# Cross attention's scores in waves of four banks, and its products in two halves of the queries

## The chip, the cores and the metric

The kernel runs on one core of one Trainium2 chip. The metric is the device time of one execution in microseconds (us). Times are medians of several runs. A profile is one execution taken by the hardware profiler. Its engines are PE (TensorE, the matrix engine; PEld is its loading of weights), DVE (VectorE), ACT (ScalarE), POOL (GpSimd) and SP (SyncE, which issues DMAs). A difference under about 0.2% (3.5 us) can't be told from none.

## What is computed

Two decoder layers over x (4 sequences, 512 positions, 256 features) with a context of 4 x 1601 x 128, all in float32. Each layer adds self attention, then cross attention, then a feed-forward block, with a layer norm behind each. The change lies in the second layer's cross attention, which has 16 heads of 16 features:

```python
qh = (q @ Wq + bq).reshape(B, LQ, HEADS, D_K).transpose(0, 2, 1, 3)
kh = (k @ Wk + bk).reshape(B, LKV, HEADS, D_K).transpose(0, 2, 1, 3)
vh = (v @ Wv + bv).reshape(B, LKV, HEADS, D_K).transpose(0, 2, 1, 3)
scores = jnp.einsum('bhqd,bhkd->bhqk', qh, kh) * scale
attn = jax.nn.softmax(scores, axis=-1)
out = jnp.einsum('bhqk,bhkd->bhqd', attn, vh)
concat = out.transpose(0, 2, 1, 3).reshape(B, LQ, D_MODEL)
return concat @ Wo + bo
```

Here `q` is x and `k`, `v` are the context, so each head has 512 queries and 1601 keys. The last feed-forward block is a tree of 255 gates and 256 leaves per position.

## The kernel before

The program has three parts, one behind the other: `front` (first layer's attentions), `experts` (first layer's feed-forward) and `heads` (the whole second layer). Each part is written as nodes of a **plan**: a node has an engine, a cost in us, a priority, the nodes it depends on and the buffers it takes. `Plan.run` is a list scheduler at build time. It keeps a model time for each engine, always places the node that can start first (within 0.05 us the one of lowest priority number), and writes the instructions in that order. So the order in each engine's queue is the plan's; the chip then waits for semaphores in that order. `hold` is a node that only takes a buffer, in turn.

For PE the plan tells three modes apart. `row` nodes are scores: a head has 16 features, padded to 32 rows of the array, and four heads lie on four row strips (lanes j = 0 to 3), so four score matmuls can run at once. `col` nodes are products of weights and values: four heads on four column strips. All other matmuls fill the whole array (`full`). `Plan.turn` (L89) decides between them: after `BURST` = 4 row nodes in a row it prefers something else, if that is ready, and after `AWAY` = 0.8 us of something else it goes back to rows.

The work is cut into groups of four heads: 4 batches x 4 groups for self attention, then as many for cross attention. `head_group` (L1050) writes one group of cross attention in two passes:

- **maxima** (L1088 to L1131). For each of 4 query tiles and each of 3 runs of 512 keys, and for each of the 4 heads, one score matmul of 32 x 512 into one PSUM bank of the pool `one` (L1098 to L1100), which DVE reduces to a maximum per query (L1106). That is 48 score matmuls and 48 reductions in a group. The 65 keys that are left go as one node of 16 small matmuls into four banks (`rest`, L1120 to L1127), with four reductions (L1129). Then the chain of the shift: the largest of them (L1134), its negative (L1137), a transpose by PE (L1142) and an addition to the queries, which makes `qa` (L1146).
- **weights and products** (L1154 to L1199). For each of 13 tiles t of keys and each of the 4 heads, one score matmul of the shifted queries into one bank (L1168), and ACT's exponential into one of ten buffers `pe` (L1173). When the four heads of a tile are there, `product` (L1187 to L1199) adds four matmuls of 512 queries to the one accumulator bank `acc` (L1190). That is 52 scores, 52 exponentials and 13 products in a group. At the end ACT copies `acc` to `o` (L1204), and PE transposes it (L1210).

The next group's exponentials depend on its own `hold` of `acc` (L1150, L1164), so the plan places them after that copy. The maxima of later groups don't depend on it.

In the program every float32 matmul is two PE instructions (two passes), so four score matmuls are 8 instructions in the profile, and so are the four matmuls of a product. All helper matmuls are recorded at L245, the products at L1190.

PSUM has eight banks here: seven in the pool `one`, one as `acc`. `one` also serves every other matmul of this part: projections of queries, keys and values (L972 to L1048), two transposes a group, and per batch the output projection with its norm (L1242, L1283) and the tree (L1333). Queries and keys go to their lanes by DMAs on SP's queue (L1066), into 2 buffers `qT` and 3 buffers `kT`.

Of the kernel before, what the change touches and what calls it, by code (L numbers as in the profile page):

```python
# [11 lines left out]
ALU = mybir.AluOpType  # L12
# [34 lines left out]
class Node:  # L47
    def __init__(self, eng, cost, prio, fn, deps, take, lanes, mode):
        self.cost = dict(zip(eng.split("|"), cost if isinstance(cost, tuple) else (cost,)))
        self.eng, self.prio, self.fn = eng, prio, fn  # L50
        self.deps, self.take, self.lanes, self.mode = deps, take, lanes, mode
        self.releases, self.users, self.slot = [], 0, None
        self.start = self.end = self.on = None


class Plan:
# [2 lines left out]

    SLACK, LOOK, BURST, AWAY, IDLE = 0.05, 96, 4, 0.8, 0.5
    LAT = {"pe": 0.25, "act": 0.1, "dve": 0.08, "pool": 0.1, "none": 0.0, "sp": 0.5, "dma": 1.5}

    def __init__(self):
# [2 lines left out]
    def pool(self, name, n):  # L68
        self.pools[name] = [0.0] * n
# [7 lines left out]
    def hold(self, name, pr, deps=()):  # L77

        before = self.turns.get(name)
        n = self.add("none", 0.0, pr, None, [*deps, *([before] if before else [])], take=[name])  # L80
        self.turns[name] = n
        return n

    def frees(self, n, those):
# [16 lines left out]
    def run(self, tc):  # L101
# [12 lines left out]
        with tc.manual_schedule():  # L114
            while todo:
                best = None
                for queue in ready.values():
                    queue.sort(key=lambda n: (n.prio, n.i))
                    options = []
                    for n in queue[: self.LOOK]:  # L120
                        s = max([d.end + self.LAT[d.on] for d in n.deps], default=0.0)
                        ok = True
                        for p in n.take:
                            times = [t for t in self.pools[p] if t is not None]
                            if not times:
                                ok = False
                                break
                            s = max(s, min(times))
                        if not ok:
                            continue  # L130
                        on = n.eng
# [22 lines left out]
                for p in n.take:  # L154
                    times = [(t, i) for i, t in enumerate(self.pools[p]) if t is not None]
                    n.slot = min(times)[1]
                    self.pools[p][n.slot] = None
                if on == "pe":
                    if n.mode == "row":
                        burst, away = burst + 1, 0.0  # L160
                    else:
                        burst, away = 0, away + n.cost[on]
                    for x in n.lanes or range(4):
                        row[x] = n.end
                    last, mode = s, n.mode
                elif on != "none":
                    free[on] = n.end
# [15 lines left out]
def cost_mm(n):  # L183

    return n * 4 / 2400


def act(n):
    return 0.1 + n * 0.833e-3


def dve(n):
    return 0.16 + n * 1.05e-3
# [11 lines left out]
def tile_decoder(ctx: ExitStack, tc: tile.TileContext, a, out):  # L205
# [38 lines left out]
    def mm(out, lhsT, rhs, c=0, n=1):  # L244
        nc.tensor.matmul(out, lhsT, rhs, start=c == 0, stop=c == n - 1)  # L245
# [666 lines left out]
    def heads():  # L912
        plan = Plan()
        with tc.tile_pool(name="h1", bufs=1) as h1, \
# [135 lines left out]
            def head_group(cross, b, g, pos, vals, pair, after):  # L1050
# [33 lines left out]
                else:  # L1084
                    for kqs in MQ:
                        units += [(j, 0, [(kq, 0, (kq + 1) * P) for kq in kqs]) for j in range(4)]
                maxes, scored = [], []
                for i, (j, m, prods) in enumerate(units):  # L1088
                    pu = pos - 1.2 + (i + 0.5) / len(units)
                    js = slice(32 * j, 32 * j + 32)  # L1090
# [10 lines left out]

                    def largest(n, s=s, j=j, m=m, at=at):
                        for kq, k0, k1, w in at:
                            t = ONE[s.slot][:, w : w + k1 - k0]
                            if cross:
                                nc.vector.tensor_reduce(MX[mx.slot][:, kq, j, m : m + 1], t, AX.X, ALU.max)  # L1106
                            else:
                                nc.vector.tensor_tensor_reduce(  # L1108
                                    out=junk[:, : k1 - k0], in0=t, in1=m_qk[:, 384 - kq * P : 512],
                                    scale=1.0, scalar=NEG, op0=ALU.add, op1=ALU.max,  # L1110
                                    accum_out=MX[mx.slot][:, kq, j, 0:1])

                    maxes.append(N("dve", sum(dve(k1 - k0) for _, k0, k1 in prods), pu, largest, [s], free=[s]))
                    scored.append(s)
                if cross:

                    pu, w = pos - 0.2, LC - 1536
                    banks = [hold("one", pu, scored[-4::]) for j in range(4)]

                    def rest(n, w=w):  # L1120
                        for kq in range(4):
                            for j in range(4):
                                js = slice(32 * j, 32 * j + 32)
                                mm(ONE[banks[j].slot][:, kq * w : (kq + 1) * w], QT[q.slot][js, kq * P : (kq + 1) * P],
                                   KT[k.slot][js, 1536:])

                    s = N("pe", cost_mm(4 * w), pu, rest, banks, lanes=(0, 1, 2, 3), mode="row")  # L1127
                    for j in range(4):
                        maxes.append(N("dve", dve(4 * w), pu, lambda n, j=j, w=w: nc.vector.tensor_reduce(  # L1129
                            MX[mx.slot][:, :, j, 3:4], ONE[banks[j].slot][:, : 4 * w].rearrange("p (a n) -> p a n", a=4),  # L1130
                            AX.X, ALU.max), [s], free=[banks[j]]))  # L1131
                pm_ = pos - 0.22
                m, nm, qa = hold("m", pm_), hold("nm", pm_), hold("qa", pm_)
                nn = N("dve", 0.2, pm_, lambda n: nc.vector.tensor_reduce(  # L1134
# [19 lines left out]
                for u, ts in enumerate(turns):  # L1154

                    at, w = [], 0
                    for t in ts:
                        at.append((t, kt_size(t) if cross else P, 0 if cross else t * P, w))
                        w += L - at[-1][2]
                    exps = []  # L1160
                    for i, j in enumerate((2, 3, 0, 1)):
                        pu = pos + (u + 0.25 * i) / len(turns)
                        js = slice(32 * j, 32 * j + 32)
                        e = hold("pe", pu, [acc])  # L1164
# [3 lines left out]
                                mm(ONE[n.slot][:kn, w : w + L - q0], KT[k.slot][js, t * P : t * P + kn], QA[qa.slot][js, q0:])  # L1168

                        s = N("pe", cost_mm(w), pu, score, [e, o, *kready], take=["one"], lanes=(j,), mode="row")  # L1170

                        def weigh(n, s=s, e=e, kn=at[0][1], w=w):
                            nc.scalar.activation(PE_[e.slot][:kn, :w], ONE[s.slot][:kn, :w], AF.Exp, scale=HD**-0.5)  # L1173

                        r = N("act", act(w), pu, weigh, [s], free=[s])
                        if not cross:
                            def causal(n, e=e, at=at):
                                for t, kn, q0, w in at:
                                    d = PE_[e.slot][:, w : w + P]
                                    nc.gpsimd.affine_select(  # L1180
                                        d, d, pattern=[[1, P]], compare_op=ALU.is_ge, fill=0.0,
                                        base=0, channel_multiplier=-1)

                            r = N("pool", len(at) * pool(128), pu, causal, [r])
                        exps.append((e, r))

                    def product(n, at=at, exps=exps, u=u):  # L1187
                        for t, kn, q0, w in at:
                            for j in range(4):
                                nc.tensor.matmul(  # L1190
                                    ACC[acc.slot][32 * j : 32 * j + HD + 1, q0:],
                                    VV[v.slot][:kn, t, 4 * (g % 2) + j, :],
                                    PE_[exps[j ^ 2][0].slot][:kn, w : w + L - q0],
                                    start=t == 0, stop=u == len(turns) - 1 and t == at[-1][0],
                                )

                    pr_ = last[-1:] if last else []
                    last.append(N("pe", cost_mm(w) + 0.05 * len(at), pos + (u + 1.2) / len(turns), product,
                                  [r for _, r in exps] + vready + [emptied] + pr_, free=[x for x, _ in exps], mode="col"))  # L1199
                plan.frees(last[-1], [k, qa])  # L1200
                if g % 2:
                    plan.frees(last[-1], [v])
# [12 lines left out]
                    RS[rs.slot], ONE[po.slot].rearrange("p (k j r) -> p k j r", k=4, j=4)[:, :, :, HD]),  # L1215
                    [po])
                if g == 0:
                    head_group.cat = hold("cat", pe_)
                cat = head_group.cat

                def scaled(n):
                    nc.vector.tensor_tensor(
# [201 lines left out]
            for k, dst in enumerate((w_gate, w_leaf)):  # L1424
                def both(n, k=k):
# [5 lines left out]
                p = N("pe", cost_mm(4 * D), 0.5, both, [fw], take=["one"], free=raw[2 * k : 2 * k + 2])  # L1431
                tree_ready.append(N("act|dve", (act(L), dve(L)), 0.5, lambda n, p=p, dst=dst: copy(
                    n.on, dst.rearrange("p m n -> p (m n)"), ONE[p.slot]), [p], free=[p]))
            pos = 0.0
            for cross in (False, True):
                for b in range(NB):
                    cats = []
                    for g in range(NG):
                        if g % 2 == 0:
                            vals = values(cross, b, g // 2, pos - 2.3, done[b])  # L1440
                            pair = projections(cross, b, g // 2, pos - 2.6, done[b])
                        c, cat = head_group(cross, b, g, pos, vals, pair, done[b])
                        cats.append(c)
                        pos += 1.0
                    done[b] = finish(cross, b, pos + 0.3, cats, cat)
                    if cross:
                        tree(b, pos + (1.2 if b < NB - 1 else 0.5), done[b])
            plan.run(tc)

    heads()  # L1450
# [99 lines left out]
```

## Time and profile before

| what | value |
|---|---|
| median of three runs | 1731.38 us (1730.46 to 1731.72) |
| the profiled execution's own time | 1728.98 us |
| its span, first to last instruction | 1727.2 us |
| mean granted PE clock | 0.974 |
| first cross score reduced by DVE (L1106) | 799.7 us |
| last cross product (L1190) begins | 1685.7 us |

The span is 1.8 us shorter than that execution's own time. The first 480 us of the span hold the first layer, up to about 799 us self attention of the second layer is the main work, and from there to 1687 us cross attention with what lies between its groups; the last 40 us are the last batch's output projection, norm and tree.

How to read the views: the page's first part gives each engine's busy time. The chain of work that ended last follows, from the last instruction back, what each step waited for; in order of time it shows how long each run of work on PE lasted, as start, length, line and count. The timeline lists instructions in order of time with the idle time before them and who ended it. The table of windows gives busy times in a stretch.

### The profile page before, as it was taken

The page shows a single profiled execution, that of the slowest core. Times are in us where ns is not written, and L with a number is a line of the kernel's source. Part 1 is how long each engine was busy: PE and PEld are TensorE (multiplying, and loading weights), DVE is VectorE, ACT ScalarE, POOL GpSimd, SP SyncE. Part 2 cuts the span into 40 slices and gives each one's busy share as a digit, 9 for nine tenths or more (in the row PEclk, how much of TensorE's full clock was granted, in tenths as well). Part 3 has the DMA queues.
Part 4 walks back from the last instruction along what each step waited for, and adds up shares of the span by engine and source line. Part 5 has one row for each costly group of instructions (what it writes and reads, how often), then busy time and mean ns, then how long its engine had stood idle before and what let it go on. Part 6 is the DMA issues. An engine that isn't in the chain of part 4 may idle for free.

```text
span 1727.2 us, 28379 instructions
## 1 busy us (share of the span) xinstructions
PE 1636.8 (95%) x10756; PEld 856.2 (50%) x10756; DVE 1104.3 (64%) x2690; ACT 759.5 (44%) x1534; POOL 330.2 (19%) x503
## 2 busy tenths in 40 slices
PE   7889999999959999999999999999999999999995
PEld 4677776888834555545433334333334333343323
DVE  6998555111138876777866766776667766677715
ACT  0335551211112434434446556455554555545581
POOL 6652003432144544422000000100000000010000
PEclk8999999999979999999999999999999999999998
DMA  8101005886331000001000000000000100001000
GB/s 304 36 2 38 25 25 199 272 277 219 115 113 38 25 14 19 17 16 26 14 3 11 14 13 14 7 19 14 13 14 1 26 14 14 13 1 26 1 1 13
DMA packets 41275, 87.50 MB, mean 51 GB/s; under 512 B 7856, under 2 KB 26800, under 8 KB 38064
## 3 DMA queue, kind: packets, MB, share of 16 engines
q1 hardware_dynamic: 32304, 42.66, 9.1%
q0 software_dynamic: 8832, 43.00, 7.3%
q8 instruction: 86, 1.41, 0.3%
q14 instruction: 53, 0.43, 0.1%
HBM read 64.52 MB, written 8.26 MB: 42 GB/s over the span
## 4 chain that ended last, share of the span: by engine, by line
PE 65%; DVE 4%; ACT 1%; issue 1%; DMA 1%; POOL 0%; DVEq 0%; POOLq 0%; ACTq 0%
PE one L245 48%; PE acc L1190 14%; DVE junk L1108 2%; PE one L1210 1%; PE one L1142 1%; PE one L1272 1%; ACT w_sgu L1173 0%; PE one L1291 0%; DMA y<-ys_dram,dest 0%; DVE x L1257 0%; DVE lst L1249 0%; DMA ys_dram<-ye 0%; PE one L1381 0%; DVE y L1308 0%; DVE rt L1373 0%
## 5 line engine op out<-in xcount | busy, mean ns | idle before, releaser
L1106 DVE TENSOR_REDUCE mx<-one 128x1 f32<-128x512 f32 x768 | 486.4, 683 | 190.0 <-PE one L245 185.7
L245 PE MATMUL one<-qa,kT 32*128 32x512 f32 (+4 forms) x2176 | 515.4, 598 | 6.2 <-ACT w_sgu L1173 4.2
L245 PE MATMUL one<-kT,qT 32*128 32x512 f32 (+4 forms) x2560 | 502.2, 529 | 6.2 <-DVE mx L1106 2.6
L1173 ACT ACTIVATE w_sgu<-one 128x512 f32<-128x512 f32 (+2 forms) x510 | 278.6, 591 | 244.8 <-PE one L245 242.7
L245 PEld LDWEIGHTS one<-qa,kT 32*128 32x128 f32 (+1 forms) x2176 | 179.6, 182 | 204.3 <-issue 68.9
L245 PEld LDWEIGHTS one<-kT,qT 32*128 32x128 f32 x2560 | 190.6, 184 | 168.3 <-issue 47.9
L1190 PE MATMUL acc<-w_sgu,v 128*17 128x512 f32 (+4 forms) x1084 | 261.9, 566 | 0.0
L1173 ACT ACTIVATE pe<-one 128x512 f32<-128x512 f32 (+1 forms) x342 | 189.8, 602 | 102.2 <-PE one L245 101.6
L1278 POOL TENSOR_TENSOR x<-x,rows 128x1024 f32<-128x1024 f32 x12 | 28.3, 2361 | 808.3 <-PE one L1272 808.2
L1190 PE MATMUL acc<-pe,v 128*17 128x512 f32 (+1 forms) x748 | 179.5, 566 | 0.0
L1108 DVE CUSTOM_DVE_ANT_0 junk<-one,consts 128x128 f32<-128x128 f32 (+3 forms) x256 | 125.4, 490 | 35.1 <-PE one L245 12.0
L1190 PEld LDWEIGHTS acc<-w_sgu,v 128*17 128x17 f32 (+1 forms) x1084 | 34.2, 96 | 176.3 <-issue 162.8
L1173 ACT ACTIVATE w_sdn<-one 128x512 f32<-128x512 f32 (+2 forms) x172 | 89.9, 568 | 63.4 <-PE one L245 63.1
L245 PEld LDWEIGHTS e_one<-xsT,wgu 128*128 128x128 f32 x768 | 89.5, 192 | 3.8 <-issue 2.9
L245 PE MATMUL e_one<-xsT,wgu 128*128 128x128 f32 x768 | 89.6, 275 | 0.0
L1190 PE MATMUL acc<-w_sdn,v 128*17 128x512 f32 (+2 forms) x344 | 84.1, 568 | 0.0
L245 PE MATMUL one<-w_in,xT 128*128 128x512 f32 (+1 forms) x128 | 47.8, 527 | 13.5 <-DMA xT<-in_xT 12.2
L245 PE MATMUL e_one<-xT,w_sgu 128*128 128x512 f32 x128 | 59.8, 609 | 0.3 <-DVE lg L613 0.3
L859 DVE TENSOR_TENSOR he<-sg,e_one 128x512 f32<-128x512 f32 x24 | 16.5, 686 | 61.6 <-PE e_one L245 51.0
L555 ACT ACTIVATE pe<-one,nm 128x512 f32<-128x512 f32 x64 | 37.3, 596 | 27.4 <-DVE nm L547 27.3
L245 PE MATMUL one<-pT,ctxN 128*128 128x128 f32 (+1 forms) x416 | 49.0, 275 | 0.0
L245 PEld LDWEIGHTS one<-pT,ctxN 128*128 128x128 f32 (+1 forms) x416 | 48.2, 192 | 1.6 <-issue 1.2
(290 smaller groups left out, 2023.3 us busy)
## 6 DMA issues: line engine op xcount, KB each, us to landing
kT<-ku SPq DMA_DIRECT2D x64, 100.1 KB
qT<-qu SPq DMA_DIRECT2D x128, 32.0 KB
ctxN<-in_ctxN SPq DMA_DIRECT2D x4, 832.0 KB
ctxT<-in_ctxT SPq DMA_DIRECT2D x4, 800.5 KB
ys_dram<-ye SPq DMA_DIRECT2D x24, 128.0 KB
xT<-in_xT SPq DMA_DIRECT2D x16, 128.0 KB
x<-in_x SPq DMA_DIRECT2D x16, 128.0 KB
x_dram<-x SPq DMA_DIRECT2D x16, 128.0 KB
```

What stands on the lines that cost most here:

```text
L245: nc.tensor.matmul(out, lhsT, rhs, start=c == 0, stop=c == n - 1)
L555: nc.scalar.activation(PE_[w.slot][:, : k1 - k0], ONE[b.slot][:, : k1 - k0], AF.Exp, bias=NM[nm.slot][:, 1:2], accum_out=PS[sm_.slot][:, i ...
L859: h = N("dve", dve(512), pr, lambda n, s=s, p=banks[1], he=he: nc.vector.tensor_tensor(HE[he.slot].rearrange("p j t -> p (j t)"), SG[s.slo ...
L1106: nc.vector.tensor_reduce(MX[mx.slot][:, kq, j, m : m + 1], t, AX.X, ALU.max)
L1108: nc.vector.tensor_tensor_reduce(out=junk[:, : k1 - k0], in0=t, in1=m_qk[:, 384 - kq * P : 512], scale=1.0, scalar=NEG, op0=ALU.add, op1=A ...
L1142: nc.tensor.transpose(ONE[n.slot][:, kq * P : (kq + 1) * P], NM[nm.slot][:, kq].rearrange("p j r -> p (j r)"), ident)
L1173: nc.scalar.activation(PE_[e.slot][:kn, :w], ONE[s.slot][:kn, :w], AF.Exp, scale=HD**-0.5)
L1190: nc.tensor.matmul(ACC[acc.slot][32 * j : 32 * j + HD + 1, q0:], VV[v.slot][:kn, t, 4 * (g % 2) + j, :], PE_[exps[j ^ 2][0].slot][:kn, w : ...
L1210: nc.tensor.transpose(ONE[n.slot][:, kq * P : (kq + 1) * P], OO[o.slot][:, kq * P : (kq + 1) * P], ident)
L1272: nc.tensor.transpose(ONE[n.slot][:, kq * P : (kq + 1) * P], XB[b][:, kq, c * P : (c + 1) * P], ident)
L1278: rw = N("pool", pool(1024), pos, lambda n: nc.gpsimd.tensor_tensor(XB[b], XB[b], rows[:, row : row + D].unsqueeze(1).to_broadcast([P, 4, ...
```

## The change

- **Waves.** Cross attention's scores are no longer nodes of one bank and one lane. A *wave* is one PE node of four score matmuls on four lanes into four banks. In the usual wave two matmuls are the shifted scores of two heads of one tile (for ACT's exponentials) of group i, and two are maxima scores of two heads (for DVE) of group i + 1 or i + 2. `head_group` becomes a generator that yields what it wants, and `wave` joins two requests.
- **The order of the waves is written out by hand**: for each group i, 18 waves of (i, i + 1), the 65 keys left of i + 1 as a wave of its own, one wave of two pairs of exponentials of i, and 6 waves of (i, i + 2). Group 0's maxima come as 12 waves of four maxima and 3 waves of group 1's; the last group's exponentials come as 13 waves of four exponentials.
- **The plan starts a wave early**: when its fourth bank will be free within 0.4 us by the plan's clock (`EARLY`). A wave counts as four of the burst.
- **Products in two halves.** In cross attention a product node is split into queries 0 to 255 and 256 to 511: two nodes of four matmuls each. The buffers `pe` are released behind the second half.
- `AWAY` is 0.4 in place of 0.8, for all plans.
- Self attention keeps its nodes. The numbers of score matmuls, reductions and exponentials are unchanged.

The diff, cut to its core:

```diff
-    SLACK, LOOK, BURST, AWAY, IDLE = 0.05, 96, 4, 0.8, 0.5
+    SLACK, LOOK, BURST, AWAY, IDLE, EARLY = 0.05, 96, 4, 0.4, 0.5, 0.4
...
+    def wave(self, cost, prio):
+        n = self.add("pe", cost, prio, None, lanes=(0, 1, 2, 3), mode="row")
+        n.parts, n.those = [], []
+        def issue(n):
+            for f, x in zip(n.those, n.parts):
+                f(x.slot)
+        n.fn = issue
+        return n
...
+                        if ok and n.parts:
+                            times = sorted(t for t in self.pools[n.parts[0].take[0]] if t is not None)
+                            ok = len(times) >= len(n.parts)
+                            if ok:
+                                s = max(s, times[len(n.parts) - 1] - self.EARLY)
...
+                for x in n.parts:
+                    p = x.take[0]
+                    t, x.slot = min((t, i) for i, t in enumerate(self.pools[p]) if t is not None)
+                    self.pools[p][x.slot] = None
+                    n.end = max(n.end, t + n.cost[on])
...
-                        burst, away = burst + 1, 0.0
+                        burst, away = burst + len(n.lanes), 0.0
...
+                if cross:
+                    for i in range(0, len(units), 2):
+                        want = []
+                        for j, m, ((kq, k0, k1),) in units[i : i + 2]:
+                            js = slice(32 * j, 32 * j + 32)
+                            want.append(lambda bank, js=js, kq=kq, k0=k0, k1=k1: mm(
+                                ONE[bank], QT[q.slot][js, kq * P : (kq + 1) * P], KT[k.slot][js, k0:k1]))
+                        s, parts = yield lambda: (want, [mx], pos - 1.2 + (i + 0.5) / len(units))
...
+                    for i in range(2 if cross else 0):
+                        pu, js2 = pos + (u + 0.5 * i + 0.25) / len(turns), (2, 3) if i == 0 else (0, 1)
...
+                        def ask():
+                            es[:] = [hold("pe", pu, [acc]) for _ in js2]
+                            return want, [*es, o, *kready], pu
+                        s, parts = yield ask
...
+                    halves = ((0, 256), (256, L)) if cross else ((0, L),)
+                    for hf, (qa0, qa1) in enumerate(halves):
...
+                        last.append(N("pe", cost_mm(w / len(halves)) + 0.05 * len(at), pos + (u + 1.2 + 0.5 * hf) / len(turns), product,
+                                      [r for _, r in exps] + vready + [emptied] + last[-1:], mode="col"))
+                    plan.frees(last[-1], [x for x, _ in exps])
...
+            AHEAD, PAIRS = 6, 24
...
+            maxima(0, PAIRS // 2)
+            wave(0, cost=cost_mm(260))
+            maxima(1, AHEAD // 2)
+            for i in range(NG * NB):
+                if i + 1 < NG * NB:
+                    for _ in range(PAIRS - AHEAD):
+                        wave(i, i + 1)
+                    wave(i + 1, cost=cost_mm(260))
+                    wave(i, i)
+                    if i + 2 < NG * NB:
+                        for _ in range(AHEAD):
+                            wave(i, i + 2)
+                    else:
+                        maxima(i, AHEAD // 2)
+                else:
+                    maxima(i, 13)
```

`cost_mm(n)` is n x 4 / 2400 us, so a wave costs 0.853 in the plan and a half of a product 0.477.

## The prediction

> **What bounds the kernel now.** I read the page first: PE is busy nearly always, the other engines are not, and the chain that ended last is PE for two thirds, nearly all of it scores (L245) and products (L1190).
>
> ```profile
> PE 1636.8 (95%) x10756; PEld 856.2 (50%) x10756; DVE 1104.3 (64%) x2690; ACT 759.5 (44%) x1534; POOL 330.2 (19%) x503
> ...
> PE 65%; DVE 4%; ACT 1%; issue 1%; DMA 1%; POOL 0%; DVEq 0%; POOLq 0%; ACTq 0%
> PE one L245 48%; PE acc L1190 14%; DVE junk L1108 2%; PE one L1210 1%; PE one L1142 1%; PE one L1272 1%; ACT w_sgu L1173 0%; PE one L1291 0%; DMA y<-ys_dram,dest 0%; DVE x L1257 0%; DVE lst L1249 0%; DMA ys_dram<-ye 0%; PE one L1381 0%; DVE y L1308 0%; DVE rt L1373 0%
> ```
>
> The table of windows puts the cross stage at 799 to 1687 us, with PE busy 878.76 of 888 us, DVE 604.68, ACT 491.37:
>
> ```profile
> 799.00:1687.00 888.00, 878.76 (x6134) 333.16 (x6126) 604.68 (x1185) 491.37 (x937) 27.13 (x57) 0.99 0.06 12
> ```
>
> But a busy PE is not a full one. The chain in order of time (start, length, what, passes) shows the pattern of a quiet stretch:
>
> ```profile
> 980.15 1.07 PE one L245 x8
> 981.23 0.98 PE acc L1190 x8
> 982.21 3.90 PE one L245 x23
> 986.11 0.98 PE acc L1190 x8
> ```
>
> Eight passes, four score matmuls on four lanes, take 1.07 us: one wave. A product takes 0.98. Then come three waves' passes (24, one of them behind the chain's cut), and they take 3.90, not 3.21. The timeline says why:
>
> ```profile
> 980.09 0.69 PE L245 MATMUL one<-qa,kT 32*128 32x512 f32 x1
> ...
> 981.24 1.09 ACT L1173 ACTIVATE w_sdn<-one 128x512 f32<-128x512 f32 x2 [1.49 <-PE one L245]
> 981.29 1.29 DVE L1106 TENSOR_REDUCE mx<-one 128x1 f32<-128x512 f32 x2 [1.14 <-PE one L245]
> ...
> 984.01 0.18 PEld L245 LDWEIGHTS one<-qa,kT 32*128 32x128 f32 x1 [0.70 <-ACT w_sgu L1173]
> ```
>
> The weight load at 984.01 waited 0.70 us for a bank: seven banks feed one wave and three quarters of the next, and a bank is free again only after ACT or DVE has drained it. I added up PE's timeline of 799 to 1687 by mode, from one run's start to the next: **rows (scores) 543 us, columns (products) 214, full 131**, together 888.
>
> **The change, part by part.** *Rows.* 48 + 52 scores in 16 groups are 1600 matmuls, 400 waves. At 1.07 each: 428. The 16 nodes of left-over keys: their 32 passes took 0.95 (1649.90 to 1650.85): 15. Rows of self attention that lie in the window, 46 passes: 6. Sum 449, against 543: **94 us of the row time is waiting**, and that is all that the change can win.
>
> *Halves.* Each of 208 products (16 x 13) becomes two. The trace has products of 256 queries, in self attention, and they take 0.56 in the chain:
>
> ```profile
> 790.49 0.56 PE acc L1190 x8
> ...
> 811.03 0.56 PE acc L1190 x8
> ```
>
> So 416 x 0.56 = 233 in place of 208 x 0.98 = 204, a cost of 29, 0.14 a product: a switch to columns and back costs the same whatever is between. Two halves that meet cost 0.98 together. How many meet? The plan puts one thing behind each wave (a wave fills the burst of 4; a half of 0.477 passes `AWAY` = 0.4). 416 waves (with the left-over ones) stand beside 416 halves and about 140 full nodes: 72 projections (9 for each of 8 pairs of groups), 32 transposes, 36 of three batch ends. So 140 things must go second into a gap, when the ten `pe` buffers run out. If these are halves: 140 x 0.14 = 20 back. I take that, 213; bound: none meet, 233. With the 10 us of columns that are self attention's and waits' today (214 less 204): **223** (bound 243).
>
> The Trainium skill has a price for this too: TensorEngine Tiling (Array Packing), section Performance Considerations, says that a matmul costs about 60 cycles beyond its columns. At the 2.4 GHz of its page TensorE: Matmul & The Clock Gate that would be, as an estimate, 25 ns, twice in a lane's half, so 10 us for 208 products in place of 29, and the result 19 us lower; the row of 0.56 is this kernel's own, and I go by it.
>
> *Bank waits that stay.* A wave that starts at 0 lets its first bank go at 1.81: ACT begins 1.15 behind the wave's start (980.09 to 981.24), one exponential lasts 0.60 (mean 604 ns), and the weight load that waits comes 0.06 later (an exponential begun at 983.36, the load at 984.01). With one half between, the next wave starts at 1.07 + 0.56 = 1.63, with three banks; its fourth lane is 0.18 late. The wave behind a late one isn't late, so the mean is 0.09 to 0.18. Gaps with a single half: 416 - 140 (a full node instead) - 140 (two halves) = 136, so 12 to 24: **18** (bound, if no halves meet: 276 gaps, 25 to 50).
>
> *Hand-over of* `acc`. The plan holds the first waves of a group until the last product is copied out. The last two halves wait for the second exponential: 1.15 + 1.09 = 2.24, where PE could go on at 1.63. The wave of left-over keys (0.95) depends on none of this and may fill it. Then two waves run with no product between, as in the 3.90: 1.81 - 1.07 = 0.74. I take 0.75 x 15 = **11**; bounds 0 (full nodes lie there) and 3.0 x 15 = 45. The upper one, if the chip keeps the plan's distance: two halves 0.98 and the copy (0.59, line below), with 0.06 for a step, end at 2.24 + 0.98 + 0.06 + 0.59 + 0.06 = 3.93; less 1.63, plus 0.74 is 3.0.
>
> ```profile
> 958.11 0.59 ACT L249 COPY o<-acc 128x512 f32<-128x512 f32 x1 [2.36 <-PE acc L1190]
> ```
>
> *DVE's long turns.* Where DVE does a batch's norm or the tree's levels (2 to 4 us in one piece), row runs are over their 1.07 a wave by 4.5 (872), 3.9 (1086), 6.1 (1329) and 3.7 (1525), and by some 8 in the first 40 us, where group 0's 48 reductions are alone. Every usual wave needs two banks from DVE, so I keep these, and 4 for smaller ones: **30** (bounds 8 and 60).
>
> *Otherwise.* Full work 131 stays. DVE drains two banks in 1.29 and ACT in 1.09, both under 1.63, so neither becomes the bound in the quiet stretches. The loads of `kT` and `qT` on SP's queue are as many, of the same buffers, some 20 waves ahead of their use; nothing new waits on SP or POOL. `AWAY` also moves self attention's order; only its 256-query product is shorter than the old bound: 0, give or take 3. Behind 1687 nothing changes.
>
> *Sum:* 449 + 223 + 131 + 18 + 11 + 30 = 862, against 888: **-26**. Against the profiled execution that is 1728.98 - 26 = 1703; the runs' median lies 2.4 higher, so 1705. As a check, one quiet group (1391.9 to 1441.4, 49.5 us: rows 32.1, columns 12.8, full 4.7) comes out at 48.3, only 1.2 less. In quiet stretches the trade is nearly even: what is won per wave in waits is mostly paid for the halves. The groups at batch ends (61 to 65 us) bring more.
>
> **Rivals.** *A, the waits go altogether:* full nodes cover the hand-over, DVE keeps up at the batch ends (8 instead of 30), waits 12: 449 + 223 + 131 + 12 + 8 = 823, -65, 1666. For it: DVE is busy 605 of 888, so on average there is room. Against: its long turns are one piece, and waves tie exponentials to them that could go alone before.
>
> *B, slower: the hand-over.* Today other maxima fill PE while `acc` changes hands; in the written order every next wave holds two exponentials of the next group, so DVE, too, gets nothing. At 3.0 us a group, 45 in place of 11: 1705 + 34 = 1739. It decides from (26 + 11) / 15 = 2.5 us a hand-over on. For it: the dependency is in the code. Against: 131 us of full work can lie there.
>
> *C, no gain:* the halves seldom meet (half of the 20 back) and single gaps cost 0.18 each, for 206 gaps: 37 in place of 18. -26 + 10 + 19 = +3, 1734. That the change doesn't form waves at all is out: one node issues its four matmuls together.
>
> **How the numbers follow.** Forecast, own range 1688 to 1722: 0.46. A (1655 to 1688): 0.20. B (over 1736): 0.18. C with what lies near it (1722 to 1736): 0.16. The range leaves out the low end of A and most of B: 1660 to 1740. Within 0.2% means 1727.9 to 1734.9, about what a measurement can tell from none: half of C, 0.08. Faster: 0.46 + 0.20 and 0.04 of C = 0.70. Slower: 0.18 and 0.04 of C = 0.22.
>
> **What would show it.** Right: chain pieces of 1.07 x8 and 0.56 x8 in turn, no row run of 3 us or more in quiet stretches, weight loads that wait about 0.2 us for ACT; rows about 508 us in the cross stage, columns about 223. Wrong: halves longer than 0.6; PE idle 2 us or more ahead of L1190 and of the copy of `acc` at each group's end (B); DVE idle over 0.5 us a wave while PE waits for DVE at batch ends over 10 us each; or self attention, 480 to 799, changed by more than 3 us.

## The result and the profile after

The changed kernel takes 1743.61 us (median of four runs, 1743.09 to 1744.01). The kernel before took 1730.92 in the same comparison. The ratio is 1.0074, with an interval of 1.0045 to 1.0103: **12.7 us slower**, where 26 us faster was forecast. The profiled execution took 1743.27 us, its span is 1740.8 us.

The page of the changed kernel: busy times, then the chain by engine and by line. Matmuls are now recorded at L282, products at L1251, self attention's masked maxima at L1153.

```profile
PE 1664.2 (96%) x12420; PEld 898.7 (52%) x12420; DVE 1107.5 (64%) x2705; ACT 779.1 (45%) x1551; POOL 319.2 (18%) x471
...
PE 66%; DVE 4%; issue 1%; DMA 0%; ACT 0%; POOL 0%; DVEq 0%; POOLq 0%
```

PE bounds it as before, and no other engine has become the bound. PE has 1664 more instructions: 208 products x 8. A quiet stretch in the chain of the changed kernel, in order of time (start, length, what, passes):

```profile
941.48 1.07 PE one L282 x8
942.55 0.56 PE acc L1251 x8
943.11 1.29 PE one L282 x8
944.40 0.56 PE acc L1251 x8
944.95 1.07 PE one L282 x8
946.02 0.56 PE acc L1251 x8
946.58 2.54 PE one L282 x32
949.12 0.56 PE acc L1251 x8
```

Waves and halves alternate as the prediction drew them, and every second wave is 0.22 us late (1.29 in place of 1.07). Then comes something that was not drawn: the wave of left-over keys, 32 passes, takes 2.54 us. The prediction priced it at 0.95.

To see how the cross stage as a whole stands, I take two marks: the start of DVE's first reduction of a cross score, and the start of the copy of `acc` to `o` for the last group of cross attention. In the kernel before they lie at 799.7 and 1686.4, so this is the stretch that the prediction added up by mode. In each kernel of the table 3740 or 3741 row passes and 657 to 660 full ones start between the marks, so the work is the same. The left column says which kernel; the experiments below are listed beside the two kernels, and each is described in its place.

| us | first cross reduction at | rows | columns | full | between the marks |
|---|---|---|---|---|---|
| before | 799.7 | 542.6 | 213.0 | 131.1 | 886.7 |
| the forecast | 799.7 | 508 | 223 | 131 | 862 |
| after | 808.6 | 525.2 | 236.3 | 129.7 | 891.2 |
| after, left-over keys interleaved | 817.1 | 499.4 | 234.4 | 129.7 | 863.5 |
| the same, and `AWAY` by stage | 797.7 | 499.5 | 234.4 | 128.7 | 862.6 |

The first mark of the changed kernel is the start that DVE's view of these reductions gives:

```profile
L1134 DVE TENSOR_REDUCE mx<-one x768: 627/681/693, 808.6 to 1658.7; 128x1 f32<-128x512 f32 x192
```

Rows fell by 17.4 where 35 was forecast, and columns rose by 23.3 where 10 was forecast: the cross stage is 4.5 us longer. Self attention, which the prediction had at "0, give or take 3", ends 9 us late by the first mark; the copy of `acc` of its 15th group, too, starts at 822.2 in place of 811.7. The two make up 13.4 of the 13.6 us by which the span grew. (The 16th copy moved only from 842.0 to 843.5; work of both stages runs side by side there.) So there were two suspects that the forecast had priced at nothing or almost: the left-over wave and `AWAY`. The rivals were B (the hand-over of `acc`) and C (halves that don't meet, longer bank waits).

### The profile page after: what moved, and what is told of

Read it like the earlier page. It is cut to its first block, busy times and chain, and to the rows that moved or that the text cites. A ratio compares the mean times of both kernels' runs of the same rounds, so it can differ in the third digit from the quotient of the medians.

```text
span 1740.8 us, 31758 instructions
## 1 busy us (share of the span) xinstructions
PE 1664.2 (96%) x12420; PEld 898.7 (52%) x12420; DVE 1107.5 (64%) x2705; ACT 779.1 (45%) x1551; POOL 319.2 (18%) x471
## 4 chain that ended last, share of the span: by engine, by line
PE 66%; DVE 4%; issue 1%; DMA 0%; ACT 0%; POOL 0%; DVEq 0%; POOLq 0%
PE one L282 48%; PE acc L1251 15%; DVE junk L1153 2%; PE one L1272 1%; PE one L1186 1%; PE one L1334 1%; PE one L1353 1%; DMA y<-ys_dram,dest 0%; DVE x L1319 0%; PE one L1443 0%; DVE lst L1311 0%; DVE lsd L1300 0%; DVE lsd L1301 0%; DVE lsd L1302 0%; POOL y L1383 0%
## 5 line engine op out<-in xcount | busy, mean ns | idle before, releaser
L282 PE MATMUL one<-kT,qT 32*128 32x512 f32 (+4 forms) x2560 | 580.2, 538 | 2.1 <-DVE mx L1153 1.8
L282 PE MATMUL one<-qa,kT 32*128 32x512 f32 (+4 forms) x2176 | 521.5, 608 | 2.4 <-DVE mx L1153 1.3
L1207 ACT ACTIVATE w_sgu<-one 128x512 f32<-128x512 f32 (+2 forms) x510 | 272.1, 586 | 210.2 <-PE one L282 210.1
L1251 PE MATMUL acc<-w_sgu,v 128*17 128x256 f32 (+4 forms) x1916 | 293.6, 394 | 1.2 <-ACT w_sgu L1207 1.2
L282 PEld LDWEIGHTS one<-qa,kT 32*128 32x128 f32 (+1 forms) x2176 | 161.5, 183 | 186.4 <-issue 125.9
L282 PEld LDWEIGHTS one<-kT,qT 32*128 32x128 f32 x2560 | 226.9, 186 | 47.8 <-issue 18.4
L1251 PEld LDWEIGHTS acc<-w_sgu,v 128*17 128x17 f32 (+1 forms) x1916 | 66.5, 96 | 300.7 <-issue 266.6
L1251 PE MATMUL acc<-pe,v 128*17 128x256 f32 (+4 forms) x1304 | 200.4, 399 | 0.0
L1153 DVE CUSTOM_DVE_ANT_0 junk<-one,consts 128x256 f32<-128x256 f32 (+3 forms) x256 | 125.4, 490 | 38.2 <-PE one L282 15.7
L1251 PE MATMUL acc<-w_sdn,v 128*17 128x256 f32 (+2 forms) x620 | 93.5, 387 | 0.0
L282 PEld LDWEIGHTS e_one<-xsT,wgu 128*128 128x128 f32 x768 | 89.5, 192 | 3.8 <-issue 2.9
L282 PE MATMUL e_one<-xsT,wgu 128*128 128x128 f32 x768 | 89.6, 275 | 0.0
L282 PE MATMUL e_one<-xT,w_sgu 128*128 128x512 f32 x128 | 59.8, 608 | 0.3 <-DVE lg L650 0.3
L282 PE MATMUL one<-w_in,xT 128*128 128x512 f32 (+1 forms) x128 | 49.1, 539 | 10.2 <-DMA xT<-in_xT 10.2
L282 PE MATMUL one<-ctxT,q 128*128 128x512 f32 (+1 forms) x128 | 49.5, 518 | 0.0
L282 PEld LDWEIGHTS one<-pT,ctxN 128*128 128x128 f32 (+1 forms) x416 | 48.2, 192 | 1.6 <-issue 1.2
```

What stands on the lines that cost most here:

```text
L1153: nc.vector.tensor_tensor_reduce(out=junk[:, : k1 - k0], in0=ONE[s.slot][:, w : w + k1 - k0], in1=m_qk[:, 384 - kq * P : 512], scale=1.0, ...
L1207: return N("act", act(w), pu, lambda n: nc.scalar.activation(PE_[e.slot][:kn, :w], ONE[x.slot][:kn, :w], AF.Exp, scale=HD**-0.5), [s], fre ...
L1251: nc.tensor.matmul(ACC[acc.slot][32 * j : 32 * j + HD + 1, max(q0, qa0) : qa1], VV[v.slot][:kn, t, 4 * (g % 2) + j, :], PE_[exps[j ^ 2][0] ...
```

## The experiments

A kernel's ratio is to the kernel before, run on the same chip, with its 95% interval. Differences between two experiments are worked out from their ratios and 1731 us.

**1. Left-over keys interleaved.** In the kernel before, one node issued the 16 matmuls of the 65 left keys with the query tile in the outer loop and the head in the inner one, so four lanes ran side by side. In the changed kernel the wave calls one closure per head, and each closure loops over the query tiles: one lane's four matmuls come in series, then the next lane's. The edit restores the old order:

```diff
-                    want = []
+                    want, banks = [], []
...
-                        def rest(bank, w=w, js=slice(32 * j, 32 * j + 32)):
-                            for kq in range(4):
-                                mm(ONE[bank][:, kq * w : (kq + 1) * w], QT[q.slot][js, kq * P : (kq + 1) * P],
-                                   KT[k.slot][js, 1536:])
+                        def rest(bank, w=w, j=j, banks=banks):
+                            banks.append(bank)
+                            for kq in range(4 if j == 3 else 0):
+                                for i, x in enumerate(banks):
+                                    js = slice(32 * i, 32 * i + 32)
+                                    mm(ONE[x][:, kq * w : (kq + 1) * w], QT[q.slot][js, kq * P : (kq + 1) * P],
+                                       KT[k.slot][js, 1536:])
```

> The changed kernel, but the 16 matmuls of the left-over keys of a group go lane by lane in turn (query tile outside, head inside), as before, and not head by head. In the changed kernel's chain these 32 passes take 2.55 us a group, before they took 0.95. Theory (the order of these matmuls is lost time on PE): 16 x 1.6 = 26 us less, 1718. Rival (the halves and their waits are the loss, and DVE's four reductions of 1.43 to 1.9 us behind these matmuls would bound them anyway): under 8 us less, 1736 or more.

Measured: 0.9935 (0.991 to 0.9959), 1714.04 us. Against the changed kernel that is 0.0139 x 1731 = **24 us less**. The timeline shows the same wave in the changed kernel:

```profile
902.92 2.47 PEld L282 LDWEIGHTS one<-kT,qT 32*128 32x128 f32 x32 [0.42 <-issue]
902.93 2.62 PE L282 MATMUL one<-kT,qT 32*128 32x65 f32 x32
904.06 1.43 DVE L1173 TENSOR_REDUCE mx<-one 128x4 f32<-128x260 f32 x3 [0.23 <-PE one L282]
```

in the kernel before:

```profile
1649.90 1.12 PE L245 MATMUL one<-kT,qT 32*128 32x65 f32 x32
```

and in this experiment:

```profile
1049.98 1.20 PEld L282 LDWEIGHTS one<-kT,qT 32*128 32x128 f32 x32 [0.42 <-issue]
1049.98 1.34 PE L282 MATMUL one<-kT,qT 32*128 32x65 f32 x32
```

The same 32 passes into the same four banks take 2.62, 1.12 and 1.34 us. The weight loads span the whole time in both orders (2.47 and 1.20). My reading is that a lane that must load, multiply, load again has nothing beside it when its neighbours come later in the queue; that the order is the cause is shown by this experiment and the next. From their first pass to the next work on PE, the 16 waves took 40.7 us in the changed kernel and 18.7 here, so 22 us lie in these waves themselves. The table has the sum: rows 525.2 to 499.4. (This experiment's runs spread from 1711.94 to 1724.19 us. The profiled one took 1724.07; its self attention, 480 to 800 us, had a clock of 0.89, so I read only the time behind the first mark from it. The 24 us are certain to some 6 only, by the two intervals; between the marks the difference is 28.) The Trainium skill, TensorEngine Tiling (Array Packing), section Tiling Modes, says that different tiles can load weights and multiply in parallel; the 1.12 agrees, and the 2.62 adds the order in which the queue must hold them for that.

**2. The same order in the kernel before.** The mirror image: its two loops swapped, nothing else.

```diff
-                        for kq in range(4):
-                            for j in range(4):
+                        for j in range(4):
+                            for kq in range(4):
```

> The kernel before with one edit: the left-over keys' matmuls go head by head, as in the changed kernel; all else as before. Theory (the order of these matmuls is lost time on PE): 16 x 1.6 = 26 us more, 1757. Rival (hidden behind DVE): under 8 us more.

Measured: 1.0198 (1.0181 to 1.0215), 1762.79 us, 34 us more: the sign as expected, and 8 us beyond the size. The 16 nodes themselves took 40.9 us in place of 22.1, waits included, so some 19 of the 34 lie in them. The granted clock was lower too, 0.97 in place of 0.99 over 800 to 1650 us, worth at most about 0.02 x 850 = 17 us. That it makes up the rest is not shown. It was lowest in a part of the cross stage; windows of this experiment and then of the kernel before (the clock is the third number from the right):

```profile
840.00:880.00 40.00, 39.32 (x216) 17.50 (x214) 25.43 (x57) 15.55 (x30) 0.29 (x1) 0.85 0.07 12
```

```profile
840.00:880.00 40.00, 39.01 (x232) 17.13 (x234) 30.11 (x66) 16.90 (x32) 0.00 (x0) 0.95 0.07 12
```

**3. `AWAY` back to 0.8, all else as changed.**

```diff
-    SLACK, LOOK, BURST, AWAY, IDLE, EARLY = 0.05, 96, 4, 0.4, 0.5, 0.4
+    SLACK, LOOK, BURST, AWAY, IDLE, EARLY = 0.05, 96, 4, 0.8, 0.5, 0.4
```

> The changed kernel with AWAY back at 0.8. Group 0's first cross reduction starts at 808.6 in the changed kernel, at 799.7 before. Theory that AWAY disturbs self attention's order: self attention and its hand-over are 9 us shorter, about 1734, and the first cross reduction is back near 800. Rival (the waves themselves, which need four banks at once, start late): no change within 3 us. In the cross stage the plan would put more than one thing between two waves; if that makes halves meet, another few us less.

Measured: 1.008 (1.0059 to 1.0101), 1743.89 us, nothing won as a whole. But the marks show two effects that cancel. The copy of `acc` of the 15th self group starts at 810.6 in place of 822.2 (811.7 before), and the first cross score reaches DVE at 797.9 in place of 808.6. Between the marks it takes 903.1 in place of 891.2. So 0.4 costs self attention 11 us and gives cross attention's waves 12.

**4. `AWAY` 0.4 in the kernel before.** The same constant alone, in the old code.

> The kernel before with AWAY 0.4, nothing else. Theory: self attention gets 10 us longer, its fifteenth copy of the accumulator comes near 822 instead of 811.7, and the whole takes 8 to 12 us more, ratio about 1.006, unless the cross stage gives it back. Rival: AWAY matters only together with waves, ratio within 0.002 of 1.

Measured: 1.0256 (1.0217 to 1.0294), 1773.69 us, 44 us more, over three times what was expected. Self attention pays here too: the first cross reduction starts at 808.0 in place of 799.7. But the cross stage of old nodes pays more: 925.7 us between the marks, against 886.7. So 0.4 is good for waves of four and bad for nodes of one, and one number for all stages doesn't serve both.

**5. `AWAY` by stage.** Experiment 1, with 0.8 until the plan places its first wave, 0.4 from there on.

```diff
-    SLACK, LOOK, BURST, AWAY, IDLE, EARLY = 0.05, 96, 4, 0.4, 0.5, 0.4
+    SLACK, LOOK, BURST, AWAY, IDLE, EARLY = 0.05, 96, 4, 0.8, 0.5, 0.4
...
+                if n.parts:
+                    self.AWAY = 0.4
```

> The kernel with the left-over keys' matmuls in turn, and AWAY at 0.8 until the plan places the first wave, 0.4 from there on. With AWAY 0.8 throughout, the fifteenth copy of the accumulator in self attention came at 810.6, with 0.4 at 822.2, but the cross stage lost 12 us. Theory (AWAY 0.4 hurts self attention and helps cross attention): 9 to 11 us less than with 0.4 throughout, ratio to before about 0.988. Rival (what self attention gains is waited for again in cross attention): no change, ratio 0.9935.

Measured: 0.9848 (0.9821 to 0.9876), 1704.26 us; against experiment 1, 0.0087 x 1731 = **15 us less**. (Experiment 1's own spread bears on this: by the two medians, 1714.04 and 1704.26, it is 10, and by the first mark of experiment 3 it is 11.) With both edits the change brings 0.0152 x 1731 = 26 us, the size of the forecast. What self attention loses at 0.4 stands in the chain by line, 555 to 790 us, first of the changed kernel, then of this experiment (where masked maxima are L1155):

```profile
by line: PE one L282 63.0%; DVE junk L1153 14.4%; PE acc L1251 9.2%; PE one L1272 3.0%; PE one L1186 2.6%; issue 2.5%; PE one L1334 1.9%; PE one L1353 1.3%; DVE mx L1153 0.6%; DVEq L1153 0.4%; ACT q L1005 0.3%; DVE qa L1190 0.3%; ACT xT L28
```

```profile
by line: PE one L284 67.1%; PE acc L1256 12.1%; DVE junk L1155 6.5%; PE one L1277 3.2%; PE one L1191 2.7%; PE one L1339 2.3%; issue 1.4%; PE one L1358 1.3%; ACT q L1007 0.6%; DVE y L1375 0.6%; ACT w_sgu L1212 0.5%; DVE qa L1195 0.3%; ACT ku
```

By the code of the plan, at 0.4 scores of self attention are preferred sooner. The chain goes through DVE's masked maxima for 14.4% of 235 us (34 us) in place of 6.5% (15 us). The clock is lower as well. Over 480 to 800 us it is 0.96 in the profiles of all seven kernels whose self attention has 0.8, and 0.89 to 0.94 in those of the six with 0.4. The chain of the changed kernel in order of time:

```profile
720.87 0.69 DVE junk L1153
...
721.71 0.69 DVE junk L1153
...
727.63 6.33 PE one L282 x10
733.97 0.56 PE acc L1251 x8
734.52 5.21 PE one L282 x42
```

and its windows there:

```profile
720.00:728.00 8.00, 7.64 (x48) 3.38 (x46) 6.93 (x27) 0.77 (x2) 3.28 (x8) 0.78 0.05 12
728.00:734.00 6.00, 6.00 (x14) 2.22 (x17) 1.23 (x6) 1.37 (x2) 1.36 (x2) 0.72 0.11 27
734.00:740.00 6.00, 6.00 (x53) 3.62 (x52) 1.39 (x2) 3.45 (x7) 4.75 (x7) 1.00 0.00 1
```

Up to 722.4 us PE is fed one masked maximum at a time. Then the clock falls to 0.78 and 0.72, and ten passes take 6.33 us. Over the last 80 us of self attention the two kernels compare so, the changed one first:

```profile
720.00:800.00 80.00, 78.11 (x551) 40.90 (x548) 52.11 (x195) 30.41 (x64) 27.66 (x77) 0.94 0.07 17
```

```profile
720.00:800.00 80.00, 77.92 (x602) 42.33 (x601) 55.79 (x210) 36.31 (x76) 24.68 (x82) 1.00 0.09 20
```

The changed kernel has 51 PE instructions fewer in the same 80 us, at 0.94 of the clock in place of 1.00. For the stretch of the two chains, 555 to 790 us, the windows are these, the changed kernel first again:

```profile
555.00:790.00 235.00, 229.81 (x1618) 120.73 (x1613) 166.31 (x619) 92.95 (x195) 95.15 (x229) 0.97 0.07 18
```

```profile
555.00:790.00 235.00, 229.92 (x1702) 121.58 (x1694) 175.84 (x650) 97.61 (x203) 98.77 (x247) 1.00 0.09 20
```

The clock can hold at most about 0.03 x 235 = 7 us of the loss. How much is the waiting itself and how much the clock, no run here separates.

**6. Whole products.** The changed kernel without halves.

```diff
-                    halves = ((0, 256), (256, L)) if cross else ((0, L),)
+                    halves = ((0, L),)
```

> The changed kernel with products whole (512 queries) in cross attention. Theory (halves are what keeps two waves apart): of two waves one follows the other directly and waits 0.74 for a bank, so two waves cost 1.07 + 0.98 + 1.07 + 0.74 = 3.86 in place of 1.07 + 0.56 + 1.29 + 0.56 = 3.48: up to 0.38 x 12 x 16 = 73 us more in quiet stretches, less where full nodes stand between: 1775 to 1815. Rival (halves are a net loss of 29 us): 1715 to 1730.

Measured: 1.0282 (1.0225 to 1.0339), 1773.59 us, 36 us more than the changed kernel and at the low edge of what was expected. Between the marks columns fall to 215.0 and rows rise to 574.2: with 13 products for some 25 waves of a group, two waves must follow each other, and the second waits.

```profile
1007.15 0.98 PE acc L1251 x8
1008.13 2.92 PE one L282 x16
1011.05 0.98 PE acc L1251 x8
```

16 passes take 2.92 in place of 2.14. Waves need halves between them.

**7. Halves in the kernel before.** The product code of the changed kernel, and nothing else of it.

```diff
+                    halves = ((0, 256), (256, L)) if cross else ((0, L),)
+                    for hf, (qa0, qa1) in enumerate(halves):
...
-                    last.append(N("pe", cost_mm(w) + 0.05 * len(at), pos + (u + 1.2) / len(turns), product,
-                                  [r for _, r in exps] + vready + [emptied] + pr_, free=[x for x, _ in exps], mode="col"))
+                        last.append(N("pe", cost_mm(w / len(halves)) + 0.05 * len(at), pos + (u + 1.2 + 0.5 * hf) / len(turns), product,
+                                      [r for _, r in exps] + vready + [emptied] + last[-1:], mode="col"))
+                    plan.frees(last[-1], [x for x, _ in exps])
```

> The kernel before with one part of the change alone: cross attention's products in two halves (single-bank scores, AWAY 0.8, left-over keys in turn, all as before). Theory (halves are worth something only where waves are written so that one stands between two of them; here AWAY 0.8 lets the plan put both halves one behind the other): ratio 0.998 to 1.006, most halves meet in runs of 16 passes at 0.98. Rival (halves by themselves cover the waits for banks): ratio 0.99 or less. Rival (each half costs its 0.14 in full): 208 x 0.14 = 29 us more, ratio 1.017.

Measured: 1.0181 (1.013 to 1.0231), 1761.66 us, 31 us more. I had expected halves to meet in the old order; they don't. Of its column runs in the cross stage 311 are of one half and 37 of two. Without waves the halves only cost. That 31 / 208 = 0.15 us a product is near the prediction's 0.14 is in part chance: between the marks columns rise by 20 (213.0 to 232.9) and rows by 13 (542.6 to 555.7). The 20 fit the row of 0.56: there are 150 column runs more than before, at 0.14 each 21 us. The rows' 13 were in no sum. The Trainium skill's 60 cycles a matmul (TensorEngine Tiling (Array Packing), section Performance Considerations) came to 10 us in the prediction's estimate; the columns alone took 20.

**8. Half exponentials.** To price the bank waits: experiment 1 with ACT's exponential over 256 of 512 queries.

```diff
+                        wd = 256 if cross else w
...
-                            PE_[e.slot][:kn, :w], ONE[x.slot][:kn, :w], AF.Exp, scale=HD**-0.5), [s], free=[x])
+                            PE_[e.slot][:kn, :wd], ONE[x.slot][:kn, :wd], AF.Exp, scale=HD**-0.5), [s], free=[x])
```

> The kernel with the left-over keys' matmuls in turn, but each exponential of cross attention takes only the first 256 of its 512 queries; the products read old values for the others. Work left out: half of ACT's elements there. It measures the wait of every second wave for a bank (1.29 instead of 1.07): an exponential of 256 frees its bank about 0.27 earlier than one of 512. Theory (that wait is on the path): the runs of 8 passes go to 1.07 throughout, 30 to 36 us less than with whole exponentials, ratio to before 0.973 to 0.977. Rival (DVE's reductions would then be the wait): under 10 us less, 0.988 or more.

Measured: 0.9755 (0.9725 to 0.9786), 1685.37 us, 0.018 x 1731 = 31 us less than experiment 1. Its chain in a quiet stretch:

```profile
1010.17 1.08 PE one L282 x8
1011.25 0.56 PE acc L1255 x8
1011.81 1.07 PE one L282 x8
1012.88 0.56 PE acc L1255 x8
1013.43 1.08 PE one L282 x8
```

The 1.29 is gone here. The runs of one wave exceed 1.07 each by 13.4 us in all here, and by 36.5 in experiment 1. So the late fourth lane was ACT's time on a bank, as the prediction had it. The fall in these runs is 23 of the 31 us; the rest I didn't trace.

**9. The hand-over of** `acc`. Rival B. Experiment 5, in which a wave no longer waits for `acc`; the products wait for it themselves.

```diff
-                            es[:] = [hold("pe", pu, [acc]) for _ in js2]
+                            es[:] = [hold("pe", pu) for _ in js2]
...
-                                      [r for _, r in exps] + vready + [emptied] + last[-1:], mode="col"))
+                                      [r for _, r in exps] + vready + [emptied, acc] + last[-1:], mode="col"))
```

> The kernel with AWAY by stage and left-over keys in turn, where the buffers of the exponentials no longer depend on the hold of the accumulator; the products depend on it instead. So the plan may place the next group's waves before the accumulator is copied. Theory (the hand-over of the accumulator costs some 0.75 us a group, in two waves with nothing between and in waits for exponentials): 5 to 12 us less than with the dependency, ratio 0.978 to 0.982. Rival (full nodes already cover it): within 3 us, 0.983 to 0.987.

Measured: 0.9799 (0.9751 to 0.9846), 1696.18 us. Against experiment 5 that is 0.0049 x 1731 = 8 us, less than the two intervals together can tell; from the start of the first cross group's copy of `acc` to the last one it takes 762.4 and then 755.7, 6.7 us less. Experiment 5's chain at a hand-over, then this one's:

```profile
993.23 2.98 PE one L284 x12
996.22 2.15 PE acc L1256 x32
998.36 1.07 PE one L284 x8
999.43 0.59 PE one L1277 x4
1000.02 2.92 PE one L284 x16
```

```profile
991.29 2.98 PE one L284 x12
994.28 0.56 PE acc L1256 x8
994.83 1.18 PE one L284 x8
996.01 0.56 PE acc L1256 x8
```

The last four halves came in one run of 32 passes, and two waves behind them had nothing between (2.92 for 16 passes). Now they alternate. A price of 7 to 8 us for 15 hand-overs is 0.5 us each, not 3.0. Of the versions that leave no work out this has the lowest median, and it beats both kernels.

**10 and 11. `EARLY`.** Experiment 1 with `EARLY` 0, and experiment 5 with 0.8 in place of 0.4.

```diff
-    SLACK, LOOK, BURST, AWAY, IDLE, EARLY = 0.05, 96, 4, 0.4, 0.5, 0.4
+    SLACK, LOOK, BURST, AWAY, IDLE, EARLY = 0.05, 96, 4, 0.4, 0.5, 0.0
```

> The kernel with the left-over keys' matmuls in turn, and EARLY 0: the plan starts a wave only when all four banks are free by its clock. Theory (the order on PE hardly depends on it, since a half lies behind every wave anyway): within 5 us of the one with EARLY 0.4, ratio to before 0.991 to 0.996. Rival (without it the plan puts full nodes and second halves ahead of waves, so halves meet): halves in runs of 16 become common, rows' waits shrink, and the time falls by 8 us or more; or PE idles and it rises by as much.

> The kernel with AWAY by stage and left-over keys in turn, and EARLY 0.8 in place of 0.4. EARLY 0 in place of 0.4 cost 0.5%. Theory (the plan's clock lets the first bank of a wave go 0.88 behind the wave's end, and with 0.4 no wave is held back any more in quiet stretches, where a half of 0.48 and two switches of 0.1 lie between): no further gain, within 3 us, ratio 0.983 to 0.987. Rival (at batch ends DVE's long turns still push waves back in the plan): 4 us or more less.

Measured: with 0, 0.9981 (0.9961 to 1.0), 1724.7 us, 8 us more than experiment 1, where less than 5 was expected. With 0.8, 0.9831 (0.9788 to 0.9875), 1702.49 us, no difference from experiment 5. The 8 us of the former lie in the cross stage: 872.6 us between the marks in place of 863.5. The cause was not tried.

## Why the prediction was wrong

**It fell on two edits, not on the waves.** Forecast -26; the left-over keys' order +24 (experiment 1 takes it away, experiment 2 puts it into the old kernel); `AWAY` in self attention +15 (experiment 5). The sum is +13, and +12.7 was measured. This is no independent check: the two prices are the two steps from the changed kernel to experiment 5, so the sum comes out because experiment 5 came out at the forecast. The +15 was measured with the left-over wave mended, and each of the two prices is certain to some 6 us (24 to 28 and 10 to 15, by the readings above); their sum is the better known, 39 us from the changed kernel to experiment 5.

**The step "The 16 nodes of left-over keys: their 32 passes took 0.95 [...]: 15"** failed. The row is right for most of the nodes in the old code. I priced the node by its count of instructions and never compared the two loop nests; in the changed kernel the 16 waves took 40.7 us (2.55 each), 26 more than the 15. The order could be read in the code of the change.

**The step "`AWAY` also moves self attention's order; [...] 0, give or take 3"** failed: self attention ended 9 us late, and with 0.8 it was back at 797.9 (experiment 3). The premise was wrong in its own terms. Not only the 256-query product costs less than the old bound: the plan's transposes, at 0.46, also lie between 0.4 and 0.8 (L1142, L1210 and others of the kernel before). And I looked at which nodes are shorter than the bound, not at what a lower bound does to the order: rows come sooner, and these rows need DVE's masked maxima, which the chain of the kernel before already showed as its third term. That the loss goes by these maxima is read from the chain; the lower clock is the other part, and the two were not separated.

**Inside the wave's sum** the total held with `AWAY` by stage, 862.6 us between the marks against the forecast's 862. That is luck, since the terms cancel:

| term | forecast | measured | from |
|---|---|---|---|
| columns | 223 | 234 to 236 | 58 halves met another, not 140 |
| bank waits | 18 | about 32 | excess of single-wave runs over 1.07, long ones left out |
| hand-over | 11 | 7 to 8 | experiment 9 |
| DVE's long turns | 30 | 5 to 8 | single-wave runs over 1.4 |

The waits were counted as 0.09 to 0.18 for 136 gaps. PE has 0.22 in every second of some 320 gaps with one half by itself, 0.11 x 320 = 35: the price was right, the number of gaps was not, since it hung on the 140. The 140 full nodes seldom pushed two halves together: 56 gaps hold full work alone, and a half often shares its gap with a full node. DVE's turns were carried over from the row runs of the old order; in the new order they hardly show. Why they shrank so far was not tried.

**Rivals.** Of A's terms, DVE keeping up came true (5 to 8 against its 8), but bank waits of 32 against its 12 and columns 11 over kept it out of reach; experiment 8 shows that the waits hang on ACT's time on a bank. B named the right side for the wrong reason: at 0.5 us a hand-over it stays far below the 2.5 from which it decides. C's two conditions came true, halves that seldom meet and longer waits; but DVE's turns, 22 to 25 us less than forecast, and the hand-over, 3 to 4 less, made up for them.

**What held:** PE as the bound, 0.56 for a half, 1.07 and 0.56 in turn, the fourth lane late for ACT (by 0.22, not 0.18). Rows were 525 in the changed kernel against the forecast's 508: the left-over wave put back more than DVE's turns gave.

## What to carry to other kernels

When a node is split into closures, compare the loop nests before and after: in this kernel matmuls on separate lanes ran side by side only where the queue held them lane by lane in turn (1.12 against 2.62 us). When a change alters a constant of a scheduler that all stages share, price it in the stages that the change does not name, by what their chain waits for, and give the constant a scope. Splitting a product pays in one order (between waves, 36 us net) and costs in another (31 us without waves), so test a part alone and in its company.

## What the runs showed of the hardware

32 passes of 65 columns on four lanes took 1.12 to 1.34 us in turn and 2.62 us lane after lane, the same matmuls in another order. The granted clock fell where PE was recorded as nearly always busy: 0.78 at 720 to 728 us with PE busy 7.64 of 8.00, and 0.72 in the 6 us behind it with 6.00 of 6.00. The Trainium skill, TensorE: Matmul & The Clock Gate, section Part 1: The HAM clock gate (the "warmup" mystery), ties the half clock to an idle window of about 3.4 us; the fall here came without such a gap in PE's recorded busy time, after a thin stretch in which the chain went from one masked maximum of DVE to the next (720.0 to 722.4 us).
